# A two-layer graph kernel issued in a hand-written order: new due times for every step, and the last bias row added to the residual on GpSimd

## The chip, the core and the metric

The kernel runs on one core of a Trainium2 chip. Five engines work beside each other, each through its own queue of instructions in order: TensorE (PE in the profile, with its weight loads shown apart as PEld), VectorE (DVE), ScalarE (ACT), GpSimd (POOL) and SyncE (SP), which here only issues transfers. They wait for each other by semaphores. The metric is the device time of one execution in microseconds, lower is better.

## The reference, cut to what matters

128 graphs of 128 nodes with 64 features each pass through two layers. Both end in a layer normalization of the layer's input plus the layer's output.

```python
# layer 0: x (128, 128, 64), adj (128, 128, 128)
mask = (adj > 0.0).astype(x.dtype)
W1a, W1b = (W1[:F], W1[F:])                      # F = 64, H = 192, O = 64
diff = x[:, :, None, :] - x[:, None, :, :]
h = relu((x @ W1a)[:, :, None, :] + diff @ W1b + b1)
hm = jnp.einsum('bjkh,bjk->bjh', h, mask)
x = _layernorm(x + hm @ W2 + deg[..., None] * b2)
# layer 1
agg = jnp.einsum('bmn,bnd->bmd', adj, x)
h = elu(agg @ W1 + b1)
h = elu(h @ W2 + b2)
x = _layernorm(x + h @ W3 + b3)
```

The names W1 to W3 and b1 to b3 of layer 1 are v1, v2, v3 and c1, c2, c3 in the kernel.

## The kernel before

**Tiling.** A round handles one pair of graphs; there are 64 rounds (p = 0 to 63), and several are in flight at once. In each graph the nodes are sorted by their number of neighbours, so that a block of similar nodes needs the same number of neighbour slots. There are nine blocks (units) for a pair. For each unit ACT copies the node's own part into one of four PSUM banks e (L910), TensorE adds the neighbours' part by 18 bf16 matmuls with a one-hot matrix oh, alternating between the two halves of the array's columns (the gather, L920), and DVE reduces the absolute values into sums (L930). The gathers are 162, 66, 168, 112, 168, 154, 169, 154 and 170 columns wide; they are called by these widths here.

**Steps of a round on TensorE, with their lines.** Transposes of adj and x (turn, L690 and L691; ACT copies the result to turned, L695). The spread of the degrees (prepare, L248 or L246; DVE ranks them at L568 and makes the permutation permb at L575). The sorting of the mask (L246, copied by ACT to mtp and permT, L659 and L661) and its prefix sums (L248 with the operand prefix, copied by ACT to vp, L668), from which DVE makes the nine oh (L675). The sorting of x (L592, copied to xsT, L596), the node's own projection (L606, copied with its bias to aj by three ACT instructions, L613) and a short correction (L626, L629, used by DVE at L635 for ea). The neighbour projection (L708 with the bias matmul L711), split into three bf16 terms cp by ACT, DVE and POOL (L718 to L727). Then finish, the chain that closes a pair: POOL subtracts a correction (hm, L842), TensorE projects (L847, L851), ACT copies ys (L855), TensorE undoes the sorting (L864), norm makes x1 = the normalized result of layer 0; layer 1 follows with L871 (copied to agg, L875), L880, elu, L886, elu, and last (L891, L893), whose result goes through norm again to the output o and its transfer.

**PSUM.** Four banks e serve the gathers. Four banks m serve all other steps in turn; a step takes the bank that came free first, so its first matmul also waits for the last reader of that bank.

**norm and last.** norm adds the residual `rest` to the PSUM result on DVE (y, L737), takes bn_stats (st, L742), has POOL make the factors (ve, rs and, for layer 0, nb; L749 to L753) and ACT apply them (L771). In layer 1 the bias c3 is not part of rest. The matmul L891 adds it in PSUM: a matrix of ones times rowp, where rowp holds the row c3 (twice, with its mean removed) as three bf16 terms on three partitions. The f32 row itself, on all partitions, is the tile rows.

**What sets the order.** Nobody waits for a scheduler at run time: the program is written in the order in which the class Flow emits it, and each engine executes its part in this order. Every step belongs to a thread (prepare, sort_x, sort_mask, turn, project_c, finish, unit), and has a due time in the table DUE, in units of a model's microseconds from the beginning of its round; a round's beginning is ROUND * p with ROUND = 11.1651. While the gathers are under way (all units except the last 14), Flow emits of all threads' next steps the one with the earliest due time:

```python
            if self.under_way:
                t, th = min(ready, key=lambda r: self._rank(r[1]))
```

For the first steps and the last 14 units it takes the step that its clock model finds ready first. A step is a tuple of engine, cost, events to come after, number of banks m, and the function that emits it. The costs move only that clock; they aren't waited for on the chip. SP issues the loads of a pair four rounds ahead (AHEAD), and the output.

Of the kernel before, what the change touches and what calls it, by code (L numbers as in the profile page):

```python
# [31 lines left out]
F32 = mybir.dt.float32  # L32
# [154 lines left out]
def sparse(tc, env):  # L187

    g = type("env", (), dict(env))
    nc, P, N, F, H, O, HB, H1, NP, E = (  # L190
        g.nc, g.P, g.N, g.F, g.H, g.O, g.HB, g.H1, g.NP, g.E)
    LAY, NB = g.LAY, g.NB
    loads, prep, work, ps_m = g.loads, g.prep, g.work, g.ps_m
# [9 lines left out]
    AHEAD = 4  # L203

    DUE = {
        "prepare": (-42.67, -37.79, -37.67, -37.41, -37.15),
        "sort_x": (-21.11, -18.03, -15.85, -13.03, -12.9, 2.76, 2.89, 3.02, 3.14),
        "sort_mask": (-28.04, -27.66, -27.27, -15.21, -14.95, -14.31, -14.05, -13.8, -13.54,
                      -13.28, -3.02, -2.76, -2.5, -2.25),
        "turn": (-38.05, -37.92),  # L210
        "project_c": (-31.63, -29.71, -29.58, -29.45, -29.32, -17.13, -13.15),
        "finish": (12.51, 20.73, 21.24, 21.37, 21.5, 21.88, 22.01, 27.91, 28.3, 28.68, 32.02,
                   34.97, 35.1, 35.23, 41.26, 41.39, 43.95, 44.08, 46.78, 46.91, 54.48, 54.61,
                   59.48),
        "unit": [(0.06, 0.19, 0.32), (0.83, 0.96, 1.09), (0.45, 0.58, 0.71), (2.37, 2.5, 2.63),
                 (3.27, 3.4, 3.53), (4.43, 4.56, 4.68), (4.81, 4.94, 5.07), (5.33, 5.71, 6.1),
                 (7.64, 10.97, 11.1)],
    }

    def begin_thread(name, p, gen):  # L220
# [15 lines left out]
    def dve(n):  # L236
        return 0.08 + n / 960
# [12 lines left out]
    def flat(t):  # L250
        return t.rearrange("p s n -> p (s n)")
# [65 lines left out]
    def made(*names):  # L317
        return [event("const", name) for name in names]
# [410 lines left out]

    LATE = NP - 1  # L730

    def norm(p, yps, ev, name, rest, shift):


        y = work.tile([P, 2, O], F32, name="y", bufs=6)
        ev, = yield ("DVE", dve(2 * O), [ev], 0,
                     lambda: nc.vector.tensor_add(flat(y), yps[:, :2 * O], flat(rest)))  # L737
        flow.give(yps, ev)
        st = work.tile([P, 2, 3], F32, name="st", bufs=12)

        ev, = yield ("DVE", 0.2, [ev], 0,
                     lambda: nc.vector.bn_stats(st.rearrange("p s t -> p (s t)"),  # L742
                                                y.rearrange("p s f -> p f s")))
        ve = work.tile([P, 2], F32, name="ve", bufs=12)
        rs = work.tile([P, 2], F32, name="rs", bufs=12)
        nb = work.tile([P, 2], F32, name="nb", bufs=12) if shift else None

        def factors():
            nc.gpsimd.tensor_scalar(ve, st[:, :, 2], 1.0 / F, EPS, op0=OP.mult, op1=OP.add)  # L749
            nc.gpsimd.tensor_tensor(rs, ve, mhalf, op=OP.pow)  # L750
            if shift:
                for s in range(2):
                    nc.gpsimd.tensor_scalar(nb[:, s:s + 1], st[:, s, 1:2], rs[:, s:s + 1], -1.0,  # L753
                                            op0=OP.mult, op1=OP.mult)

        def variance():
            nc.vector.tensor_scalar(ve, st[:, :, 2], 1.0 / F, EPS, op0=OP.mult, op1=OP.add)

        def center(s):
            nc.vector.tensor_scalar(o[:, s, :], y[:, s, :], st[:, s, 1:2] if shift else 0.0,  # L760
                                    rs[:, s:s + 1], op0=OP.subtract, op1=OP.mult)
        if p < LATE:
            ev, = yield ("POOL PORT", 1.27 if shift else 0.97, [ev] + made("mhalf"), 0, factors)
        else:
            ev, = yield ("DVE", 0.1, [ev], 0, variance)
            ev, = yield ("POOL", 0.7, [ev] + made("mhalf"), 0,
                         lambda: nc.gpsimd.tensor_tensor(rs, ve, mhalf, op=OP.pow))
        o = work.tile([P, 2, F], F32, name=name, bufs=6)

        def apply(s):  # L770
            nc.scalar.activation(o[:, s, :], y[:, s, :], AF.Identity,  # L771
                                 bias=nb[:, s:s + 1] if shift else 0.0, scale=rs[:, s:s + 1])
        if p < LATE:
            ev, = yield ("ACT", 0.6 if shift else 0.46, [ev], 0, lambda: [apply(s) for s in range(2)])
        elif shift:
            ev, = yield ("DVE", 0.4, [ev], 0, lambda: [center(s) for s in range(2)])
# [25 lines left out]
    def overflow():  # L802
# [29 lines left out]
        ev, = yield ("DVE", 0.2, [ev], 0, lambda: v.tensor_reduce(some, t[:1, :B], AX.X, OP.max))  # L832
        flow.give(t, ev)

    def finish(p):

        d, xx = S[p], XX[p]
        hm = work.tile([P, 3, N], F32, name="hm")
        late = p >= LATE
        ev, = yield ("DVE PORT" if late else "POOL PORT", 0.47 if late else 1.05,  # L840
                     [event("corr", p)] + [event("sums", p, i) for i in range(NB)], 0,
                     lambda: (nc.vector if late else nc.gpsimd).tensor_sub(hm, d["sums"], d["corr"]))  # L842

        def project(yb):
            cp, mtp = d["cp"], d["mtp"]
            for c in range(3):
                nc.tensor.matmul(yb[:, :2 * O], hm[:, c, :], flat(w2d[:, c]),  # L847
                                 start=(c == 0), stop=False)
            for s in range(2):
                for i in range(3):  # L850
                    nc.tensor.matmul(yb[:, s * O:(s + 1) * O], mtp[:, s, :], cp[:, i, s, H:H + O],  # L851
                                     start=False, stop=(s == 1 and i == 2))
        ev, yb = yield ("PE", 0.85, [ev] + made("w2d"), 1, project)
        ys = work.tile([P, 2 * O], F32, name="ys")
        ev, = yield ("ACT", act(2 * O), [ev], 0, lambda: nc.scalar.copy(ys, yb[:, :2 * O]))  # L855
        flow.give(yb, ev)
        if p == NP - 1:
            due = DUE["finish"]
            flow.start(ROUND * p, [due[4]] * 4 + [due[8], due[12], due[12], due[14], due[15], due[15]],
                       overflow())  # L860

        def unsort(t):
            for s in range(2):
                nc.tensor.matmul(t[:, s * O:(s + 1) * O], d["permT"][:, s, :],  # L864
                                 ys[:, s * O:(s + 1) * O], start=True, stop=True)
        ev, t = yield ("PE", 0.4, [ev, event("permT", p)], 1, unsort)
        x1, ev = yield from norm(p, t, ev, "x1", xx, True)

        def aggregate(t):
            for s in range(2):  # L870
                nc.tensor.matmul(t[s * F:(s + 1) * F, :N], x1[:, s, :], d["turned"][:, s, :],  # L871
                                 start=True, stop=True)
        ev, t = yield ("PE:t", 0.22, [ev, event("turned", p)], 1, aggregate)
        agg = work.tile([P, N], F32, name="agg")
        ev, = yield ("ACT", act(N), [ev], 0, lambda: nc.scalar.copy(agg, t[:, :N]))  # L875
        flow.give(t, ev)

        def hidden1(zb):
            for s in range(2):
                nc.tensor.matmul(zb[:, s * N:(s + 1) * N], v1p[:, s, :], agg,  # L880
                                 start=True, stop=True)
        ev, zb = yield ("PE", 0.49, [ev] + made("v1p"), 1, hidden1)
        h1, ev = yield from elu(zb, ev, "h1", 0)

        def hidden2(zb):
            nc.tensor.matmul(zb[:, :2 * N], v2s, h1, start=True, stop=True)  # L886
        ev, zb = yield ("PE", 0.48, [ev], 1, hidden2)
        h2, ev = yield from elu(zb, ev, "h2", 1)

        def last(t):  # L890
            nc.tensor.matmul(t[:, :2 * O], onesb[:, :P], c3p, start=True, stop=False)  # L891
            for s in range(2):
                nc.tensor.matmul(t[:, s * O:(s + 1) * O], h2[:, s * N:(s + 1) * N], v3s,  # L893
                                 start=False, stop=(s == 1))
# [284 lines left out]
```

## Time and profile before

| | us |
|---|---|
| median of 3 runs | 772.05 (771.89 to 772.5) |
| the profiled execution | 772.32 |
| its span, first to last instruction | 770.6 |
| one round in the middle of the run | 11.395 |
| first gather's second matmul starts at | 30.68 |
| last gather ends, about | 749.4 |

The granted TensorE clock is 0.985 on average. The span is what the profile shows of the execution; 1.7 us lie around it. A start-to-start distance is the time from the start of one instruction to that of the next on the same engine; where neither waits, it is what the instruction costs its engine, while the duration in the profile also holds the part that overlaps the next. The matmul's end in the profile is modelled, so its start and the start of its weight load are the times to trust. An f32 matmul appears as two instructions.

Busy times of the engines in two rounds in the middle of the run, a view of stretches:

```profile
411.10:422.50 11.40, 11.40 (x235) 10.46 (x232) 11.08 (x38) 10.98 (x32) 6.62 (x13) 1.00 0.11 27
422.50:433.89 11.39, 11.39 (x235) 10.45 (x232) 11.07 (x38) 10.97 (x32) 6.61 (x13) 1.00 0.11 26
```

The columns after the window are its length, and busy time with the number of instructions for PE, PEld, DVE, ACT and POOL; then the granted clock, the share of the DMA engines and GB/s. The rounds repeat to within a few nanoseconds.

POOL's and DVE's instructions that the change is near to:

| line | what | mean ns |
|---|---|---|
| L737 | y, DVE, 128 x 128 | 275 to 286 |
| L742 | bn_stats, DVE | 289 |
| L727 | third term of cp, POOL, 128 x 512 | 1162 |
| L842, L620, L642 | f32 two-input operations, POOL, 128 x 384 | 1002 to 1021 |
| L363 | f32 subtraction, POOL, 128 x 64 | 306 |
| L891 | bias matmul, PE, 128 columns bf16 | 222 |

### The profile page before, as it was taken

What the parts mean: (1) busy time and instruction counts of PE and PEld (TensorE: products, weight loads), DVE (VectorE), ACT (ScalarE), POOL (GpSimd) and SP (SyncE); (2) the same over time, 40 slices, a digit from 0 to 9 for tenths busy, and PEclk for the clock granted to TensorE, in tenths of its full rate; (3) what the DMA queues carried; (4) which work ended last, traced back from release to release, by engine and by line L of the source; (5) the groups of instructions that cost most, each with busy time, mean ns of one, the idle gap of its engine ahead of it and who ended that gap; (6) DMA issues with size and microseconds to landing.
All of it is one profiled execution on the core that took longest, in us unless ns stands there. A gap on an engine that the chain in (4) does not pass through costs nothing.

```text
span 770.6 us, 36007 instructions
## 1 busy us (share of the span) xinstructions
PE 746.3 (97%) x14616; PEld 679.5 (88%) x14617; DVE 725.2 (94%) x2381; ACT 705.5 (92%) x1986; POOL 430.1 (56%) x801
## 2 busy tenths in 40 slices
PE   7599999999999999999999999999999999999995
PEld 5489999999999999999999999999999999999993
DVE  6699999999999999999999999999999999999994
ACT  5479999999999999999999999999999999999984
POOL 5145565565565565556556556556555655655652
PEclk9699999999999999999999999999999999999997
DMA  4000010110110011011011011011101101100000
GB/s 123 11 3 3 17 30 17 30 31 20 27 30 23 24 31 30 16 31 30 17 30 30 17 30 31 21 26 31 30 17 30 31 16 31 31 17 19 11 10 21
DMA packets 54668, 19.70 MB, mean 26 GB/s; under 512 B 37601, under 2 KB 54497, under 8 KB 54497
## 3 DMA queue, kind: packets, MB, share of 16 engines
q1 hardware_dynamic: 53792, 17.05, 9.1%
q8 instruction: 116, 1.90, 1.0%
q14 instruction: 56, 0.45, 0.2%
q10 hardware_dynamic: 704, 0.30, 0.2%
HBM read 13.14 MB, written 4.19 MB: 22 GB/s over the span
## 4 chain that ended last, share of the span: by engine, by line
PE 94%; DVE 3%; ACT 2%; issue 0%; DMA 0%; POOL 0%; ACTq 0%; POOLq 0%; DVEq 0%
PE e L920 45%; PE m L606 6%; PE m L708 5%; PE m L847 5%; PE m L880 4%; PE m L886 4%; PE m L864 4%; PE m L893 4%; PE m L690 3%; PE m L248 2%; PE m L871 2%; PE m L592 2%; PE m L246 2%; PE m L851 1%; PE m L711 1%; PE m L691 1%
## 5 line engine op out<-in xcount | busy, mean ns | idle before, releaser
L920 PE MATMUL e<-oh,cp 128*64 128x162 bf16 (+3 forms) x10368 | 392.7, 229 | 6.2 <-DVE oh L675 5.2
L920 PEld LDWEIGHTS <-cp 128*64 128x64 bf16 x10368 | 356.9, 110 | 15.3 <-issue 6.9
L930 DVE TENSOR_REDUCE sums<-e 128x54 f32<-128x486 f32 (+8 forms) x576 | 327.1, 609 | 16.7 <-PE m L629 9.9
L910 ACT COPY e<-aj 128x504 f32<-128x504 f32 (+6 forms) x576 | 293.3, 540 | 9.5 <-DVE sums L930 8.9
L749 POOL TENSOR_SCALAR ve<-st 128x2 f32<-128x2 f32 x126 | 24.1, 191 | 254.1 <-DVE st L742 246.9
L675 DVE TENSOR_TENSOR oh<-vp,slotc 128x308 bf16<-128x308 bf16 (+6 forms) x576 | 137.3, 314 | 0.8 <-ACT vp L668 0.6
L750 POOL TENSOR_TENSOR rs<-ve,mhalf 128x2 f32<-128x2 f32 x126 | 87.8, 696 | 10.5
L727 POOL TENSOR_TENSOR cp<-r,cp 128x512 bf16<-128x512 f32 x64 | 74.4, 1162 | 18.6 <-ACT cp L725 18.6
L642 POOL TENSOR_TENSOR corr<-ea,sa 128x384 f32<-128x384 f32 x64 | 64.2, 1003 | 32.8 <-DVE ea L635 32.8
L842 POOL TENSOR_TENSOR hm<-sums,corr 128x384 f32<-128x384 f32 x63 | 63.1, 1002 | 5.8 <-DVE sums L930 5.8
L620 POOL TENSOR_TENSOR sa<-aj,srow 128x384 f32<-128x384 f32 x64 | 65.4, 1021 | 0.0
L797 DVE SCALAR_TENSOR_TENSOR h<-m,cc,e 128x256 f32<-128x256 f32 x128 | 60.8, 475 | 3.8 <-ACT e L794 3.6
L791 ACT ACTIVATE r<-m,cc 128x256 f32<-128x256 f32 x128 | 61.3, 479 | 2.4 <-PE m L886 2.4
L606 PEld LDWEIGHTS m<-xsT,wad 128*128 128x128 f32 x384 | 48.3, 193 | 13.0 <-ACT turned L695 11.8
L613 ACT ACTIVATE aj<-m,b1c 128x128 f32<-128x128 f32 x192 | 57.2, 386 | 2.3 <-PE m L606 2.3
L606 PE MATMUL m<-xsT,wad 128*128 128x128 f32 x384 | 58.4, 289 | 0.6 <-DVE r L722 0.6
L794 ACT ACTIVATE e<-r 128x256 f32<-128x256 f32 x128 | 53.3, 418 | 2.0
L847 PE MATMUL m<-w2d,hm 128*128 128x128 f32 x384 | 53.4, 276 | 0.0
L722 DVE TENSOR_TENSOR r<-m,cp 128x256 f32<-128x256 f32 x128 | 47.8, 415 | 2.8 <-ACT cp L718 2.8
L771 ACT ACTIVATE x<-y,nb,rs 128x64 f32<-128x64 f32 x126 | 48.9, 439 | 1.4 <-POOL nb L753 1.4
L847 PEld LDWEIGHTS m<-w2d,hm 128*128 128x128 f32 x384 | 48.1, 192 | 0.1
L708 PE MATMUL m<-wc,turned 64*128 64x256 f32 x256 | 46.3, 436 | 0.9 <-DVE r L722 0.9
(159 smaller groups left out, 1350.5 us busy)
## 6 DMA issues: line engine op xcount, KB each, us to landing
adj<-in_adj_dram SPq DMA_DIRECT2D x64, 128.0 KB, 2.4
xx<-in_x_dram SPq DMA_DIRECT2D x64, 64.0 KB, 2.2
out_dram<-o SPq DMA_DIRECT2D x64, 64.0 KB, 1.6
w1s<-in_L_gnn_W_dram ACTq DMA_DIRECT2D x2, 96.0 KB, 2.8
w2s<-in_L_gnn_W_dram ACTq DMA_DIRECT2D x2, 48.0 KB, 2.7
v2s<-in_L_gnn_W_dram SPq DMA_DIRECT2D x1, 64.0 KB, 2.3
v1d<-in_L_gnn_W_dram SPq DMA_DIRECT2D x2, 32.0 KB, 2.0
rows<-in_L_gnn_b_dram SPq DMA_DIRECT2D x1, 64.0 KB, 4.8
```

The costliest lines, as they stand in the source:

```text
L606: nc.tensor.matmul(aps[:, c * N:(c + 1) * N], wad[:, c, :], xsT, start=True, stop=True)
L620: evs, = yield ("POOL PORT", 1.0, [have] + made("srow"), 0, lambda: nc.gpsimd.tensor_mul(sa, aj, srow))
L642: ev, = yield ("POOL PORT", 1.05, [ev, evs], 0, lambda: nc.gpsimd.tensor_sub(corr, ea, sa))
L675: lambda: nc.vector.tensor_tensor(oh[:, :, c].rearrange("p b (s w) -> p b s w", w=w), vp[:, :, p0:p1].rearrange("p b (o w) -> p b o w", o= ...
L708: nc.tensor.matmul(cps[s][:, :cols], d["turned"][k, 2, :], wc[k, :], start=True, stop=False)
L727: lambda: nc.gpsimd.tensor_sub(cp[:, 2], r1, cp[:, 1]))
L750: nc.gpsimd.tensor_tensor(rs, ve, mhalf, op=OP.pow)
L842: lambda: (nc.vector if late else nc.gpsimd).tensor_sub(hm, d["sums"], d["corr"]))
L847: nc.tensor.matmul(yb[:, :2 * O], hm[:, c, :], flat(w2d[:, c]), start=(c == 0), stop=False)
L910: lambda: nc.scalar.copy(e.rearrange("p (c s w) -> p c s w", c=3, w=w), d["aj"][:, :, p0:p1].rearrange("p c (o w) -> p c o w", o=1) .to_br ...
L920: nc.tensor.matmul(e[s * HB:(s + 1) * HB, c * n:(c + 1) * n], cp[:, k, s, c * HB:(c + 1) * HB], oh[:, s, base:base + n], start=False, stop ...
L930: nc.vector.tensor_reduce(d["sums"][:, :, p0:p1], e.rearrange("p (c s w) -> p c w s", c=3, w=w), AX.X, OP.add, apply_absolute_value=True)
```

## The change

Three parts.

1. In last, the bias matmul L891 goes; the two matmuls with v3s open and close their own groups.
2. A new thread, residual, is started as soon as x1 is known. Its one step adds rows to x1 on POOL, into a new tile x1c with 4 buffers, due at 32.7. The second norm takes x1c as its rest, and its y step waits for that event as well.
3. All due times in DUE are new, except ROUND, so every engine's instructions stand in another order.

```diff
     DUE = {
-        "prepare": (-42.67, -37.79, -37.67, -37.41, -37.15),
+        "prepare": (-43.06, -42.93, -39.21, -39.08, -35.87),
...
-        "finish": (12.51, 20.73, 21.24, 21.37, 21.5, 21.88, 22.01, 27.91, 28.3, 28.68, 32.02,
-                   34.97, 35.1, 35.23, 41.26, 41.39, 43.95, 44.08, 46.78, 46.91, 54.48, 54.61,
-                   59.48),
-        "unit": [(0.06, 0.19, 0.32), (0.83, 0.96, 1.09), (0.45, 0.58, 0.71), (2.37, 2.5, 2.63),
+        "finish": (12.64, 19.44, 19.57, 21.62, 21.75, 21.88, 22.01, 28.04, 28.17, 29.2, 33.56,
+                   33.69, 33.82, 34.71, 43.31, 43.44, 44.47, 44.6, 46.52, 46.65, 48.06, 48.19,
+                   59.87),
+        "residual": (32.7,),
+        "unit": [(-1.48, 0.96, 1.09), (2.12, 2.25, 2.37), (3.02, 3.14, 3.27), (3.66, 3.79, 3.91),
...
-    def norm(p, yps, ev, name, rest, shift):
+    def norm(p, yps, ev, name, rest, shift, *after):
...
-        ev, = yield ("DVE", dve(2 * O), [ev], 0,
+        ev, = yield ("DVE", dve(2 * O), [ev, *after], 0,
...
+    def residual(p, x1, x1c, ev):
+
+        ev, = yield ("POOL PORT", 0.45, [ev] + made("rows"), 0,
+                     lambda: nc.gpsimd.tensor_add(flat(x1c), flat(x1), rows))
+        happened(ev, "x1c", p)
...
         x1, ev = yield from norm(p, t, ev, "x1", xx, True)
+        x1c = work.tile([P, 2, F], F32, name="x1c", bufs=4)
+        flow.start(ROUND * p, DUE["residual"], residual(p, x1, x1c, ev))
...
         def last(t):
-            nc.tensor.matmul(t[:, :2 * O], onesb[:, :P], c3p, start=True, stop=False)
             for s in range(2):
                 nc.tensor.matmul(t[:, s * O:(s + 1) * O], h2[:, s * N:(s + 1) * N], v3s,
-                                 start=False, stop=(s == 1))
+                                 start=True, stop=True)
...
-        o, ev = yield from norm(p, t, ev, "o", x1, False)
+        o, ev = yield from norm(p, t, ev, "o", x1c, False, event("x1c", p))
```

The steps of one round in the middle of the run, as they stand on TensorE (named by the lines of the kernel before; gathers by their widths):

| before | after |
|---|---|
| L690, L691 | L690, L691 |
| L248 spread, L248 prefix, L886, L606 | L606 |
| L847, L851 | L847, L851 |
| L880, L864 | L886, L248 prefix, L864, L880 |
| gathers 170, 162, 168, 66 | gather 170, L592, gather 162 |
| L708, L711, L891, L893 | L708, L711, L893 |
| gather 112, L626, L629 | gather 66, L626, L629 |
| gather 168, L592, gathers 154, 169 | gathers 168, 112, 168, 154 |
| L246 sorting, gather 154, L871 | L246 spread, L871, gathers 169, 154, L246 sorting |

On POOL the new order is corr, ve and rs of the output's norm, cp, the new x1c, ve, rs and nb of x1's norm, hm, the two small degree operations, sa. On DVE one round reads: ea; sums 168; bn_stats of the output; sums 112; the two differences for cp (L722); sums 168 and 154; the two rankings; sums 169 and 154; oh for 154 and 66; permb; six more oh; oh for 162, which reads the vp just made; y of x1; its bn_stats; h2; sums 170 and 162; h1; the two mask operations (L545); y of the output; sums 66. The chain that makes rowp stays in the program, for the dense path that runs only when a pair overflows its slots.

More of the change, by code (lines that the diff above doesn't have):

```diff
@@ L205, in sparse @@
     DUE = {
-        "prepare": (-42.67, -37.79, -37.67, -37.41, -37.15),
[L207 to L211, printed above, removed]
-        "finish": (12.51, 20.73, 21.24, 21.37, 21.5, 21.88, 22.01, 27.91, 28.3, 28.68, 32.02,
-                   34.97, 35.1, 35.23, 41.26, 41.39, 43.95, 44.08, 46.78, 46.91, 54.48, 54.61,
-                   59.48),
-        "unit": [(0.06, 0.19, 0.32), (0.83, 0.96, 1.09), (0.45, 0.58, 0.71), (2.37, 2.5, 2.63),
-                 (3.27, 3.4, 3.53), (4.43, 4.56, 4.68), (4.81, 4.94, 5.07), (5.33, 5.71, 6.1),
-                 (7.64, 10.97, 11.1)],
+        "prepare": (-43.06, -42.93, -39.21, -39.08, -35.87),
+        "sort_x": (-26.76, -10.46, -10.33, -3.14, -3.02, 2.5, 2.63, 2.76, 2.89),
+        "sort_mask": (-26.12, -25.99, -25.86, -23.42, -23.29, -23.16, -13.67, -13.28, -13.03,
+                      -12.77, -2.63, -2.25, -1.99, -1.73),
+        "turn": (-36.9, -36.77),
+        "project_c": (-32.15, -29.32, -29.2, -29.07, -28.94, -4.17, -4.04),
+        "finish": (12.64, 19.44, 19.57, 21.62, 21.75, 21.88, 22.01, 28.04, 28.17, 29.2, 33.56,
[3 more added lines that the diff above has]
+        "unit": [(-1.48, 0.96, 1.09), (2.12, 2.25, 2.37), (3.02, 3.14, 3.27), (3.66, 3.79, 3.91),
+                 (4.68, 4.81, 4.94), (5.07, 5.2, 5.33), (5.97, 6.1, 6.22), (6.35, 6.48, 6.61),
+                 (7.25, 11.61, 11.74)],
     }
```

## The prediction

> **What bounds the kernel now.** I read the page first (busy times, the chain that ended last), then the waits, then the timelines of TensorE, its weight loads (PEld) and ACT over one round. A round (one pair of batches) takes 11.395 us: the same line starts again after that time in 56 of the 63 steps between rounds, from 72 to 710 us. The profiled execution took 772.32 us, 770.6 of it span.
>
> From the page:
>
> ```profile
> span 770.6 us, 36007 instructions
> ...
> PE 746.3 (97%) x14616; PEld 679.5 (88%) x14617; DVE 725.2 (94%) x2381; ACT 705.5 (92%) x1986; POOL 430.1 (56%) x801
> ...
> PE 94%; DVE 3%; ACT 2%; issue 0%; DMA 0%; POOL 0%; ACTq 0%; POOLq 0%; DVEq 0%
> ```
>
> TensorE sets the end. But busy matmuls are not matmuls at their peak: a weight load that waits is hidden behind the modelled end of the matmul before it. One such wait shows in the list of waits (total, times, longest), and the timelines of one round (start, duration, engine, line, operation, out<-in, size, count, idle before it) show two more by their starts:
>
> ```profile
> PEld m L606 <- ACT turned L695: 11.8, 57, 0.2
> ```
>
> ```profile
> 412.61 0.27 PE L248 MATMUL m<-mtp,prefix 128*128 128x256 bf16 x1
> 412.72 0.65 PE L886 MATMUL m<-h,v2s 128*128 128x256 f32 x2
> 413.21 0.91 PE L606 MATMUL m<-xsT,wad 128*128 128x128 f32 x6
> ...
> 414.62 0.34 PE L851 MATMUL m<-cp,mtp 128*128 128x64 bf16 x6
> 414.79 0.69 PE L880 MATMUL m<-agg,v1p 128*128 128x128 f32 x4
> 415.32 0.65 PE L864 MATMUL m<-ys,permT 128*128 128x64 f32 x4
> 415.90 2.44 PE L920 MATMUL e<-oh,cp 128*64 128x170 bf16 x72
> ...
> 418.97 0.22 PE L891 MATMUL m<-rowp,onesb 128*128 128x128 bf16 x1
> 419.02 0.61 PE L893 MATMUL m<-v3s,h 128*128 128x64 f32 x4
> ```
>
> ```profile
> 412.67 0.30 PEld L886 LDWEIGHTS m<-h,v2s 128*128 128x128 f32 x2
> 413.18 0.74 PEld L606 LDWEIGHTS m<-xsT,wad 128*128 128x128 f32 x6 [0.21 <-ACT turned L695]
> 415.31 0.52 PEld L864 LDWEIGHTS m<-ys,permT 128*128 128x128 f32 x4
> 418.94 0.10 PEld L891 LDWEIGHTS <-onesb 128*128 128x128 bf16 x1
> 418.97 0.53 PEld L893 LDWEIGHTS m<-v3s,h 128*128 128x128 f32 x4
> ```
>
> ```profile
> 412.35 0.27 ACT L596 COPY xsT<-m 128x128 f32<-128x128 f32 x1
> 412.64 0.48 ACT L695 COPY turned<-m 128x384 f32<-128x384 f32 x1
> 414.99 0.27 ACT L855 COPY ys<-m 128x128 f32<-128x128 f32 x1
> ```
>
> Elsewhere a load starts 2 ns after the matmul before it starts. Three loads start 0.05 us after an ACT copy ends instead. L886 waits for xsT (412.62): its two matmuls stand 270 ns apart, not the 216 of an unhindered 256-column f32 pass: 54 ns lost. L606 waits for turned (413.12): 182 ns, not 112: 70 lost. L864 waits for ys (415.26): the last matmul of L880 starts at 415.21, so 100 lost. Sum 0.224 us a round; unhindered, this order needs 11.395 - 0.224 = 11.171.
>
> **What the Trainium skill says.** "TensorE: Matmul & The Clock Gate", step-by-step part, lets the queue pull a weight load ahead of matmuls in flight; so a load costs only what is longer than the matmul it runs behind. Its section on LDWEIGHTS gives columns/1.2, 107 ns for 128; f32 loads here follow each other at 110 to 112. Its section on weight-path modes says 128-column non-f32 loads are faster; the trace has 29 (418.94 to 418.97). "SBUF — State Buffer", who interferes with whom: a VectorE instruction with two SBUF inputs and a GpSimd one that reads SBUF exclude each other for the whole instruction. The nine oh (L675) are of that kind; in the round shown POOL rests during them (oh 413.92 to 416.06, POOL idle from 412.44 to 416.36), so no run here shows the collision.
>
> **The change part by part**, per round, on TensorE.
> 1. Bias matmul gone. It streams 57 ns (418.97 to 419.02), but the 110 ns f32 load of L893 runs behind it. Without it that load starts 29 ns earlier, behind L711, and then stands bare. Nearest case: once in the drain (745.0 us) a 64-column f32 matmul follows a short bf16 one, L851 to L864, and reaches its second start 28 + 140 = 168 ns later; L711 over L891 to the second start of L893 takes 29 + 57 + 111 = 197. So 29 saved, not 57; bounds 0 (all hidden) to 57.
> 2. L880 now stands last before the gathers, not L864. Before a gather the array drains: 123 ns pass after the start of a 64-column bf16 matmul (L711, early rounds), its stream of 27 and 96 more; 205 after L864's last, which is 54 of a load still running, a stream of 53 and 98. The eight matmuls cost 112 each in either order; only the last stream lies bare, and for 128 f32 columns it is 107, not 53: +53 (bounds 0 to 60).
> 3. The spread of the degrees (L248, 3 x 56 = 168) becomes six half-width matmuls among gathers, three pairs at 57: +3. L592, L871, L626, L629 and the gathers only change places; the column streams add up as before.
> 4. The waits. The new order puts L606 right behind L691; its bank was last read by agg, whose ACT copy (my layout, below) ends 1.2 us earlier: 0. L886 moves behind L851 and waits for turned, 0.7 us early: 0. L864 gets L886 and L248 in front of it instead of L880. From the last L851 matmul its load would start 0.54 us later (110 load + 216 + 216), not 0.45; ys was ready at 0.55. Stall 0.00 to 0.01, from 0.100.
>
> Sum: 11.171 - 0.029 + 0.053 + 0.003 = 11.198; 0.197 less than 11.395, times 56 = 11.0 us. So nearly all comes from the reordering.
>
> This holds if nothing else is late. I laid one round of the new order on all engines with start-to-start distances from the trace, time 0 at L690.
> ACT: turned 0.65 to 1.12, aj behind L606 (1.26), ys 2.10, vp 3.13, xsT 4.64, then without a pause to the copy for the 169-column gather, done 9.33, needed 9.58. That 0.25 is the smallest margin of a gather.
> DVE: its 29 groups add up to 10.91, with one new own wait (bn_stats right behind its y, 0.12) inside and about 0.07 on a gather. It starts at 3.56 with oh for 162, which waits for vp, and is back there at 14.54: 0.2 spare in 11.20. h2 is done 4.85, its bank needed by L708 at 5.15; h1 6.40, needed by L626 at 6.74.
> POOL: 7.4 of 11.2. The new add of 128 elements costs 0.45 (from 64: 0.305, 384: 1.00; the page has no 128), behind cp (10.82 to 11.94), ahead of ve at 15.6. Its reader, the output y, comes at 17.9: it hides behind that 5 us. Behind it on POOL wait only ve, rs and nb. DVE's new wait for it has h1 and mk ahead of it, and the sums for the 66-column gather and all later sums behind.
> Constants: rows is f32 and made before rowp already; SP's issues keep their order; rowp and its constant chain stay for the unused dense path. The first gather still waits for all nine oh behind that chain (PE idle 4.9 us before 30.68). Fill and drain chains keep their length; I allow 1 us either way.
>
> So span 770.6 - 11.0 = 759.6, execution about 761.3; the median shown is 0.27 under the profiled execution: **761.0 us**.
>
> **Rivals.**
> A, the wait grows back: ys has no margin, aj sits ahead of it on ACT. If ys, the 169 copy or h2 are late by 0.1 a round, half is lost: 11.30, 766.7. For it: three ACT waits exist now. Against: the margins above, 0.25 except ys.
> B, slower: oh and the new add exclude each other. The add would end at 12.39 and the first oh start at 12.45, so they touch. If oh comes first, the add waits up to 2 us, which its cover of 5 us takes. Up to 0.2 of blocking DVE absorbs; from there it bounds. The whole 0.45 on top of 10.98 gives 11.43: 774.0. If cp too slid onto oh (1.16), 12.14 and 814; for that ACT would have to be 0.6 late.
> C, only the bias matmul counts and all three waits come back elsewhere: 11.198 + 0.224 = 11.42, 773.5. Against: each wait's partner was looked up in the new order.
> D, the change as described does less: 64 matmuls and loads are gone and 64 adds are there; but what the title names is worth 1.6 us (56 x 0.029), or 3.2 if I mis-sized it.
>
> **How the numbers follow.** Forecast 0.72 (own range 759.3 to 763.5: period 11.18 to 11.24, ends 1 us); A 0.12; B 0.10; C 0.06. The range 759 to 767 holds the forecast's case and most of A's; B and C, 0.16, lie above it, and some of the forecast's ends below or above its own range. A measurement of this kernel tells 0.2% (1.5 us) from no change. Faster: 0.72 + 0.12 = 0.84; of C 0.03 within, 0.03 above; B above: same 0.03, slower 0.13.
>
> **What would show it.** A period of 11.20 between starts of L606; no PEld wait at L606; no weight load that starts just after an ACT copy ends; the first two matmuls of L893 near 140 ns apart; DVE with a short wait for vp each round; POOL's new add ended before the first oh. Wrong if DVE's oh last longer or start late while POOL reads, or if L711 to L893 saves its full 57.

## The result, and the profile after

| | before | changed |
|---|---|---|
| median of the runs shown | 772.27 us | 759.66 us (759.28 to 760.08) |
| ratio, 95% interval | | 0.9835 (0.9820 to 0.9851) |
| span of the profiled execution | 770.6 us | 758.3 us |
| distance between rounds, steady | 11.395 us | 11.212 us |

The forecast was 761.0. From the page after (span, busy time of each engine, shares of the chain that ended last):

```profile
span 758.3 us, 36113 instructions
...
PE 735.9 (97%) x14724; PEld 670.9 (88%) x14725; DVE 723.3 (95%) x2381; ACT 706.4 (93%) x1986; POOL 459.6 (61%) x865
...
PE 94%; DVE 1%; DMA 1%; ACT 1%; SPq 1%; issue 0%; POOL 0%; POOLq 0%; DVEq 0%
```

TensorE still sets the end, and its busy share did not move: 97% before, 97% after. What changed stands in the starts of one round. The changed kernel has other line numbers: its L607, L709, L712, L854, L858, L895, L249, L871, L889, L880, L901 and L928 on TensorE are L606, L708, L711, L847, L851, L886, L248, L864, L880, L871, L893 and L920 of the kernel before, and its oh (L676 on DVE) is L675. From the timeline of the changed kernel (start us, duration, engine, line, operation, out<-in, size, count), TensorE's full-width stretch and the output layer:

```profile
402.77 0.83 PE L607 MATMUL m<-xsT,wad 128*128 128x128 f32 x6
403.44 0.83 PE L854 MATMUL m<-w2d,hm 128*128 128x128 f32 x6
404.11 0.34 PE L858 MATMUL m<-cp,mtp 128*128 128x64 bf16 x6
404.28 0.68 PE L895 MATMUL m<-h,v2s 128*128 128x256 f32 x2
404.80 0.27 PE L249 MATMUL m<-mtp,prefix 128*128 128x256 bf16 x1
404.91 0.56 PE L871 MATMUL m<-ys,permT 128*128 128x64 f32 x4
405.30 0.66 PE L889 MATMUL m<-agg,v1p 128*128 128x128 f32 x4
405.89 0.85 PE L928 MATMUL e<-oh,cp 128*64 128x170 bf16 x18
...
408.17 0.23 PE L712 MATMUL m<-b2p,onesb 128*128 128x64 bf16 x2
408.23 0.64 PE L901 MATMUL m<-v3s,h 128*128 128x64 f32 x4
```

The same for the weight loads, and for ACT's copies:

```profile
402.66 0.75 PEld L607 LDWEIGHTS m<-xsT,wad 128*128 128x128 f32 x6
404.25 0.30 PEld L895 LDWEIGHTS m<-h,v2s 128*128 128x128 f32 x2
404.80 0.52 PEld L871 LDWEIGHTS m<-ys,permT 128*128 128x128 f32 x4
408.21 0.53 PEld L901 LDWEIGHTS m<-v3s,h 128*128 128x128 f32 x4
```

```profile
403.02 0.50 ACT L696 COPY turned<-m 128x384 f32<-128x384 f32 x1
404.48 0.27 ACT L862 COPY ys<-m 128x128 f32<-128x128 f32 x1
407.02 0.27 ACT L597 COPY xsT<-m 128x128 f32<-128x128 f32 x1
```

The three waits are gone, but for a trace of one. L607's loads run from 402.66 with nothing to wait for: its six starts stand 558 ns apart in all (629 before), and the list of waits has no entry for a load of L607. L895's first load starts 2 ns behind the last start of L858. L871's load alone still carries the sign of a wait: it starts 51 or 52 ns behind the end of ys (404.75) in every one of 55 rounds. But this is only 2 to 7 ns behind the start of L249, so some 5 ns are lost there at most, and not 100. ys comes just in time, with nothing to spare.

POOL and DVE around the new addition, in the same round:

```profile
403.11 0.46 POOL L839 TENSOR_TENSOR x1c<-x,rows 128x128 f32<-128x128 f32 x1
403.65 0.47 DVE L676 TENSOR_TENSOR oh<-vp,slotc 128x308 bf16<-128x308 bf16 x2
```

The addition ends at 403.57, 0.08 us ahead of the first oh. In 48 of 50 rounds this gap lies between 0.05 and 0.09 us; once it is 0.15, and once there is none.

**Where the 12.3 us went.** Fifty-six steady steps of 0.183 us are 10.2 us. The rest comes from the two ends. At the start the gather that waits for all oh of the first round comes 3.1 us earlier. From the timelines of the kernel before and of the changed one:

```profile
24.14 0.15 DVE L508 TENSOR_TENSOR cc<-cc,m 128x1 f32<-128x1 f32 x1 [0.88 <-PE m L505]
...
30.68 3.14 PE L920 MATMUL e<-oh,cp 128*64 128x162 bf16 x53 [4.92 <-DVE oh L675]
```

```profile
20.21 0.15 DVE L509 TENSOR_TENSOR cc<-cc,m 128x1 f32<-128x1 f32 x1 [0.66 <-ACT e L918]
...
27.56 1.38 PE L928 MATMUL e<-oh,cp 128*64 128x162 bf16 x17 [5.57 <-DVE oh L676]
```

The wait is not shorter (in brackets: idle before, and who ended it), but the constant chain that stands ahead of the oh on DVE begins at 20.21 and not at 24.14. Where the steady rounds begin, the changed kernel leads by 4.3 us (the gather of 162 columns at 70.45 and not at 74.75), where they end by 14.5 (698.31 and not 712.85), and at the end of the span by 12.3. So the start gave 4.3 us, and 2.3 were given back behind the steady rounds.

### The profile page after: what moved, and what is told of

It is laid out like the page before. It is cut to its first block, busy times and chain, and to the rows that moved or that the text cites. A ratio compares the mean times of both kernels' runs of the same rounds, so it can differ in the third digit from the quotient of the medians.

```text
span 758.3 us, 36113 instructions
## 1 busy us (share of the span) xinstructions
PE 735.9 (97%) x14724; PEld 670.9 (88%) x14725; DVE 723.3 (95%) x2381; ACT 706.4 (93%) x1986; POOL 459.6 (61%) x865
## 4 chain that ended last, share of the span: by engine, by line
PE 94%; DVE 1%; DMA 1%; ACT 1%; SPq 1%; issue 0%; POOL 0%; POOLq 0%; DVEq 0%
PE e L928 47%; PE m L607 6%; PE m L854 6%; PE m L709 5%; PE m L895 4%; PE m L889 4%; PE m L901 4%; PE m L871 3%; PE m L247 3%; PE m L691 3%; PE m L880 2%; PE m L593 2%; PE m L858 1%; PE m L712 1%; PE m L692 1%; PE m L249 1%
## 5 line engine op out<-in xcount | busy, mean ns | idle before, releaser
L928 PE MATMUL e<-oh,cp 128*64 128x162 bf16 (+3 forms) x10368 | 393.2, 229 | 6.0 <-DVE oh L676 5.6
L928 PEld LDWEIGHTS <-cp 128*64 128x64 bf16 x10368 | 357.7, 110 | 18.6 <-issue 6.9
L938 DVE TENSOR_REDUCE sums<-e 128x54 f32<-128x486 f32 (+8 forms) x576 | 334.1, 608 | 7.6 <-PE e L928 4.3
L676 DVE TENSOR_TENSOR oh<-vp,slotc 128x308 bf16<-128x308 bf16 (+6 forms) x576 | 149.4, 315 | 4.5 <-ACT vp L669 0.9
L607 PE MATMUL m<-xsT,wad 128*128 128x128 f32 x384 | 53.7, 276 | 0.0
L854 PE MATMUL m<-w2d,hm 128*128 128x128 f32 x384 | 53.5, 275 | 0.0
L719 ACT CAST cp<-m 128x256 bf16<-128x256 f32 x128 | 40.2, 365 | 8.7 <-PE m L712 8.7
L607 PEld LDWEIGHTS m<-xsT,wad 128*128 128x128 f32 x384 | 47.9, 192 | 0.3
L854 PEld LDWEIGHTS m<-w2d,hm 128*128 128x128 f32 x384 | 48.0, 192 | 0.1
```

The source lines that it names most:

```text
L607: nc.tensor.matmul(aps[:, c * N:(c + 1) * N], wad[:, c, :], xsT, start=True, stop=True)
L676: lambda: nc.vector.tensor_tensor(oh[:, :, c].rearrange("p b (s w) -> p b s w", w=w), vp[:, :, p0:p1].rearrange("p b (o w) -> p b o w", o= ...
L928: nc.tensor.matmul(e[s * HB:(s + 1) * HB, c * n:(c + 1) * n], cp[:, k, s, c * HB:(c + 1) * HB], oh[:, s, base:base + n], start=False, stop ...
L938: nc.vector.tensor_reduce(d["sums"][:, :, p0:p1], e.rearrange("p (c s w) -> p c w s", c=3, w=w), AX.X, OP.add, apply_absolute_value=True)
```

## The experiments

To keep starts and ends apart from the rounds, each profile is cut in three: the start of the gather of 162 columns in round 5 (counted from 0), the mean distance of rounds 5 to 55, and the stretch from this gather in round 55 to the end of the span. First + 50 x distance + last is the span.

| kernel | median us | ratio to before, 95% | round 5 | distance | behind round 55 |
|---|---|---|---|---|---|
| before | 771.7 to 772.3 | 1 | 86.14 | 11.395 | 114.71 |
| changed | 759.66 | 0.9835 (0.9820, 0.9851) | 81.66 | 11.212 | 116.08 |
| old_order_add | 773.65 | 1.0017 (1.0010, 1.0023) | 85.68 | 11.365 | 117.75 |
| new_order_bias | 758.89 | 0.9837 (0.9824, 0.9851) | 80.69 | 11.240 | 114.16 |
| h1_before_unsort | 756.35 | 0.9789 (0.9770, 0.9807) | 82.20 | 11.158 | 115.55 |
| rows_late | 759.43 | 0.9845 (0.9832, 0.9859) | 81.12 | 11.212 | 115.97 |
| old_order_h2_late | 792.94 | 1.0270 (1.0256, 1.0284) | 87.17 | 11.724 | 118.33 |
| h2_late_behind_copy | 764.69 | 0.9905 (0.9890, 0.9921) | 85.33 | 11.228 | 115.92 |
| add_thrice | 760.30 | 0.9838 (0.9824, 0.9851) | 81.45 | 11.223 | 116.69 |
| add_six | 811.75 | 1.0512 (1.0497, 1.0526) | 82.89 | 12.063 | 124.98 |
| tail_bias | 759.08 | 0.9835 (0.9821, 0.9848) | 80.53 | 11.212 | 115.32 |
| rowp_spread | 757.63 | 0.9813 (0.9800, 0.9827) | 79.17 | 11.212 | 116.13 |
| old_consts_early | 769.49 | 0.9971 (0.9958, 0.9984) | 83.74 | 11.394 | 114.18 |
| swap_rowp | 753.72 | 0.9763 (0.9750, 0.9777) | 78.38 | 11.158 | 115.68 |

The distances repeat to some 3 ns from round to round, but for a few rounds of the two kernels with more additions. The column of round 5 and the last one carry 1 to 2 us of chance; what the runs show of its reason is said at the end.

### The two halves of the change, each alone

old_order_add takes the table of due times of before, with a place for the addition behind cp, and only what the title says of the bias row (the title's part, below):

```diff
+        "residual": (31.65,),
...
-            nc.tensor.matmul(t[:, :2 * O], onesb[:, :P], c3p, start=True, stop=False)
...
-        o, ev = yield from norm(p, t, ev, "o", x1, False)
+        o, ev = yield from norm(p, t, ev, "o", x1c, False, event("x1c", p))
```

> The old order on every engine, with only the title's part: no bias matmul L891, the bias row added to the residual by POOL right behind cp, x1c read by the output y. Theory (a removed bias matmul saves the 29 ns by which L893's first load starts earlier): period 11.366 us instead of 11.395, 64 x 0.029 = 1.9 us less, 770.4 against 772.3. Rival (its whole 57 ns counts): 3.6 us less, 768.6. Rival (the title's part carries the gain and the order only accompanies it): near 760.

new_order_bias is the changed kernel with these lines put back and without the addition.

> The new order on every engine, with the bias matmul kept and no addition on POOL. Theory (the order carries the gain): period 11.212 + 0.029 = 11.241 us, 1.9 us over the changed kernel, 761.5. Rival (57 ns): 763.3. Rival (the title's part carries the gain): near 771.

The distances came out at 11.365 and 11.240: the bias matmul is worth 29 ns in the old order and 28 in the new one, not its stream of 57. The times did not follow. old_order_add is slower than before by 0.17%, and new_order_bias no slower than the changed kernel: what the title's part saves in the rounds (1.6 us) does not reach the end of the profiled executions, where the last column grows by 3.0 us in the old order and by 1.9 in the new one. So the gain of the change is the order's; in the medians of whole runs the title's part is worth nothing, or a little less. In the new order this comparison isn't a clean one, though. Four of the five runs of new_order_bias had a mean granted clock of 0.988 or 0.989 (758.59 to 759.26 us) and the fifth 0.983 (761.09), while all four of the changed kernel had 0.983 or 0.984 (759.28 to 760.08). At a like clock the changed kernel is 1.0 to 1.8 us faster, by that one run.

### The order alone: taking away the waits by one move

old_order_h2_late leaves everything of before in place but hidden2 (L886), which goes between L880 and L864, and its relu on ACT, which goes right behind ys:

```diff
-                   34.97, 35.1, 35.23, 41.26, 41.39, 43.95, 44.08, 46.78, 46.91, 54.48, 54.61,
+                   34.97, 35.1, 35.23, 43.25, 43.6, 43.95, 44.08, 46.78, 46.91, 54.48, 54.61,
```

> The kernel before with one thread's step moved: L886 (hidden2) between L880 and L864 instead of ahead of L606, its relu behind ys on ACT; bias matmul, spread of the degrees and all else as before. Theory (the three hidden weight-load waits are what the new order removes): L606 takes over the bank that xsT frees and keeps the 54 ns wait for xsT, L847 takes the bank that turned frees and comes after it, L864 comes 0.4 us after ys is ready: 0.170 of the 0.224 us go, period 11.225 us, 772.0 - 56 x 0.170 = 762.5. Rival (the waits only move to the next line that takes the bank): 11.39 and 772. Rival (the h2 chain, now 1.4 us later, makes L893 wait): above 772.

It was slower than before: 11.724, and for a reason that none of the three expectations has. On TensorE the expected happened (the starts of L847 stand 558 ns apart, those of L864 279 where it was 375, and only L606 keeps a wait of 50 for xsT). But in the timeline of ACT stands a wait that was not there:

```profile
413.15 0.29 ACT L855 COPY ys<-m 128x128 f32<-128x128 f32 x1
414.02 0.47 ACT L791 ACTIVATE r<-m,cc 128x256 f32<-128x256 f32 x1 [0.58 <-PE m L886]
```

relu comes to the head of ACT's queue 0.58 us before L886 is done, and the copies for the next gathers are queued behind it. ACT is busy for 11.04 us of this round and has no 0.58 us to give, so it became the bound. The second attempt puts relu one copy later, and the two steps behind it with it:

```diff
-                   34.97, 35.1, 35.23, 41.26, 41.39, 43.95, 44.08, 46.78, 46.91, 54.48, 54.61,
+                   34.97, 35.1, 35.23, 43.25, 44.76, 44.8, 44.84, 46.78, 46.91, 54.48, 54.61,
```

> As old_order_h2_late, which lost because h2's relu, put right behind ys, held ACT idle for 0.58 us a round until L886 was done; here relu and exp stand behind the copy for the 162-column gather, one copy later on ACT, so that L886 is done when they come. Theory (ACT had no room for the wait; the three TensorE waits themselves are worth what the trace shows): ACT does not wait at relu, period 11.225 to 11.26 us, 762 to 765. Rival (the h2 chain or a gather copy is late wherever relu stands): above 11.395, 772.

11.228, against 11.225 worked out from the two waits. So these two hidden waits are worth what the starts in the profile of before say, and taking them away needs a few steps of one thread moved and nothing else of the change. The third, the one for xsT, was not taken away alone: here L606 keeps some 50 ns of it, and it goes only in the changed kernel.

### What stands last before the gathers

h1_before_unsort is the changed kernel with one due time made earlier, so that L889 (hidden1) comes ahead of L871 (the unsorting):

```diff
-        "finish": (12.64, 19.44, 19.57, 21.62, 21.75, 21.88, 22.01, 28.04, 28.17, 29.2, 33.56,
+        "finish": (12.64, 19.44, 19.57, 21.62, 21.75, 21.88, 22.01, 28.04, 28.17, 29.2, 32.75,
```

> The changed kernel with L889 (hidden1) moved ahead of L871 (unsort) on TensorE, nothing else moved. Theory (the last matmul before the gathers lies bare with its stream, 107 ns for 128 f32 columns, 53 for 64): period 11.212 - 0.053 = 11.159 us, 3.0 us less, 756.7. Rival (the unsort's result, 0.4 us later, makes DVE's y late, or DVE has no room left below 11.21): period 11.21, 759.7, with a DVE wait at y. Rival (the drain does not depend on what stands last): 759.7 with the gap before the gather unchanged at 205 ns and no DVE wait.

11.158, 54 ns less. From the first start of these eight matmuls to the gather pass 986 ns in the changed kernel and 933 here. Read by the starts of the matmuls, the difference lies not behind the last start (205 ns to the gather either way) but inside L889, whose four starts stand 389 ns apart in the changed kernel and 335 here. The starts of the loads put it back in its place. A start in the record can come before the matmul's own load is done: L871's second start in the changed kernel stands 58 ns behind its first, while its load began 3 ns behind that first start and needs some 110. Counted with 110 ns a load, which is an estimate from the distances of the loads, the last load before the gather ends 1 ns behind the last start in the changed kernel (load at 405.578, start at 405.687) and 55 ns behind it here (404.625 and 404.680). That leaves 204 and 150 ns to the gather: a stream of 107 or of 53, and 97 more in both. DVE's y has no wait. This is the 53 ns that the change had paid for its order.

### Does the addition collide with the oh?

add_thrice and add_six repeat the addition with the same inputs and output:

```diff
-                     lambda: nc.gpsimd.tensor_add(flat(x1c), flat(x1), rows))
+                     lambda: [nc.gpsimd.tensor_add(flat(x1c), flat(x1), rows) for k in range(6)])
```

> The changed kernel with the new addition on POOL done three times in a row (same inputs, same output), so that 1.37 us of POOL instead of 0.457 stand from the end of cp, 0.9 us of them beside the first oh of DVE. Theory of rival B in the prediction (a DVE instruction with two SBUF inputs and a POOL instruction that reads SBUF exclude each other): the first oh last 0.4 to 0.5 us longer each where they meet an addition, 0.9 us of DVE lost, of which 0.15 to 0.25 is covered by its wait for vp: period 11.85 to 11.95, 796 to 801 us. Other theory (they only share bandwidth, or not even that): oh as long as before, period 11.212, 759.7.

> The changed kernel with POOL's new addition done six times. In add_thrice the two additions that met the oh cost DVE 0.31 us (oh of 66 columns 496 ns instead of 236, of 169 columns 383 instead of 338), and DVE's wait for vp took up all but 0.01. Theory (each waits for the other to end, and DVE has 0.15 to 0.25 us to give): five additions beside the oh cost DVE 0.8 us or more, period 11.75 or more, 790 or more. Rival (the loss is taken up by other waits too): period below 11.3, 765 or less.

Three additions left the distance at 11.212 in 47 of the 50 rounds; the mean is 0.011 higher because three rounds are 0.11, 0.15 and 0.30 us longer, and the cause of these is open. Yet the collision was there in every round: the oh of 66 columns took 0.50 us and not 0.24, the one of 169 columns 0.38 and not 0.34, and the addition beside the first 0.60 instead of 0.46. DVE lost 0.31 us a round and gave it from its own waits, that for vp (0.15) among them. Six additions lengthened five oh by 1.19 us together, more than DVE had to give: 12.063, 0.85 more. From the groups of DVE by shape (two batches of columns each, so 132 are 66), of add_six and then of the changed kernel (busy us, mean ns of one):

```profile
L676 DVE TENSOR_TENSOR oh<-vp,slotc 128x224 bf16<-128x224 bf16 x64 | 35.8, 560 | 0.0
L676 DVE TENSOR_TENSOR oh<-vp,slotc 128x132 bf16<-128x132 bf16 x64 | 31.2, 488 | 0.0
...
L676 DVE TENSOR_TENSOR oh<-vp,slotc 128x340 bf16<-128x340 bf16 x64 | 21.3, 332 | 0.0
```

```profile
L676 DVE TENSOR_TENSOR oh<-vp,slotc 128x340 bf16<-128x340 bf16 x64 | 21.2, 331 | 0.0
...
L676 DVE TENSOR_TENSOR oh<-vp,slotc 128x224 bf16<-128x224 bf16 x64 | 18.1, 284 | 0.0
L676 DVE TENSOR_TENSOR oh<-vp,slotc 128x132 bf16<-128x132 bf16 x64 | 15.6, 244 | 0.0
```

An oh that meets an addition lasts 0.04 us (169 columns) to 0.30 us longer; one that comes after the last addition (340) is as before. For three, the first theory had the mechanism right and the size wrong (0.65 to 0.75 expected, 0.01 measured): an addition cost DVE at most 0.3 us, not its whole 0.46, and DVE has room for 0.3. For six its 11.75 or more held.

### The start

rows_late spreads the last fourteen DVE instructions of the constant chain over rounds 1 and 2 instead of ahead of the first oh:

```diff
+        flow.start(14.0, range(14), consts_rows(c3, ev))
+
+    def consts_rows(c3, ev):
```

> The changed kernel, with the last fourteen DVE instructions of the constant chain (means of v3s and rows, the bf16 parts of rowp; 3.2 us of DVE from 22.89 to 26.09) spread behind the first oh instead of ahead of them. Theory (the start of the changed kernel is 3.7 us earlier than before because this chain begins earlier, and the rest of its length still holds the first gathers): the gather that waits until 27.56 starts 3.2 us earlier, 759.7 - 3.2 = 756.5, period unchanged at 11.212. Rival (something else, the cp planes or the second pair's sort, holds the first gathers at that time): 759.7.

The gather did start at 23.92, 3.6 us earlier, and the gathers of round 2 still 3.8 earlier (45.20 against 48.98), but those of round 3 only 0.5: round 2 took 13.97 us (10.74 in the changed kernel). So the time stayed at 759.43, as the rival had it, though not for the rival's reason. Seven of the moved instructions stand in round 2, where DVE is busy for 13.75 us. They take 3.4 us there and 1.6 at the start of the changed kernel: about half of the loss is that DVE has no room for them, the other half that three of them met POOL. The timelines of POOL and DVE of this kernel show two of these:

```profile
48.22 1.00 POOL L853 TENSOR_TENSOR hm<-sums,corr 128x384 f32<-128x384 f32 x1
...
49.52 0.99 POOL L625 TENSOR_TENSOR sa<-aj,srow 128x384 f32<-128x384 f32 x1
```

```profile
48.40 0.96 DVE L366 TENSOR_TENSOR low<-hm,mid 128x128 bf16<-128x128 f32 x1
...
49.56 1.00 DVE L367 COPY rowp<-hi 1x128 bf16<-1x128 bf16 x1
```

At the start of the changed kernel, beside an idle POOL, low took 0.29 us and the copy of one row 0.18. Here each lasts to just behind the end of the POOL instruction that it meets. rowp_spread moves only the seven instructions of rowp, one a round into rounds 8 to 14, ahead of the last oh, where DVE waits for vp and POOL rests. For this one of their scratch tiles gets memory of its own, x1c has 3 buffers and not 4, and only the last five pairs still wait for rowp:

```diff
-        for name, fn in parts(rows, rowp, NR):
+        flow.start(10.0, [ROUND * k for k in range(8, 15)], consts_rowp())
```

> The changed kernel, with only the seven DVE instructions that make rowp (which no matmul of the sparse path reads any more) moved from the start to rounds 8 to 14, one a round, into DVE's wait for vp ahead of the last oh, where POOL rests. Theory (they hold the first gathers, and beside the oh they cost nothing): the second gather starts 1.6 us earlier, period 11.212 but for up to 0.1 us in seven rounds, 758.1 to 758.5. Rival (time won ahead of the first gathers is lost again in rounds 1 and 2, as it was when the whole chain was spread there): 759.7.

The waiting gather starts at 25.52 and not at 27.56, the distance stays 11.212, and the gain lasts to the end: 757.63. That the beginning of the chain matters as much as its length was tried on the kernel before, by its due time alone:

```diff
-    flow.start(ROUND * -0.5, [0.0], consts_late())
+    flow.start(ROUND * -1.2, [0.0], consts_late())
```

> The kernel before, with the constant chain (sums of the weights on TensorE, then the DVE chain to rowp) placed earlier by its due time, so that its two matmuls stand ahead of a pair of L708 that waits for DVE and no longer behind it; from round 2 on nothing differs. Theory (the start is shorter in the changed kernel because this chain begins 3.9 us earlier): the wait of the first gathers ends 3.0 to 3.5 us earlier than at 30.68, period 11.395, 768.6 to 769.2. Rival (the new place of the units and sorts in the first rounds makes the difference): 772.

The chain begins at 20.66 and the gather starts at 28.89 (30.68 before), at an unchanged distance: 2.2 us less in the medians, 3.0 in the spans. 1.8 of the expected 3.0 to 3.5 show at the gather itself. The chain begins 3.5 us earlier, but from its begin to the first oh behind it pass 5.4 us and not 4.6, because two of its instructions meet POOL:

```profile
23.27 1.15 POOL L727 TENSOR_TENSOR cp<-r,cp 128x512 bf16<-128x512 f32 x1 [4.91 <-ACT cp L725]
23.40 1.10 DVE L364 CAST mid<-hm 128x128 bf16<-128x128 f32 x1
...
24.38 0.99 POOL L642 TENSOR_TENSOR corr<-ea,sa 128x384 f32<-128x384 f32 x1
24.54 0.98 DVE L365 TENSOR_TENSOR low<-hm,mid 128x128 bf16<-128x128 f32 x1
```

In the kernel before mid takes 0.23 us and low 0.29, and one instruction of the chain meets POOL (L510, 0.91 us). The other 0.9 us go to an oh and two r that had run ahead of the chain and now stand behind it.

### The end, and the two that paid together

tail_bias lets the last five pairs add their bias row by the matmul again.

```diff
+        with_matmul = p >= NP - 5
...
+            if with_matmul:
+                nc.tensor.matmul(t[:, :2 * O], onesb[:, :P], c3p, start=True, stop=False)
```

> The changed kernel, but the last five pairs add the bias row by the matmul as before and not on POOL. Theory (the title's part saves 29 ns in each of the steady rounds, and gives 2 to 3 us back after them, where TensorE's granted clock falls to half about 5 us earlier): period 11.212, the stretch behind the last steady round 2 us shorter, 757.6. Rival (the 2 us were chance of one execution): 759.7.

This one decides nothing: its runs lie between 757.65 and 760.10 and cover both expectations.

swap_rowp joins h1_before_unsort and rowp_spread.

> The changed kernel with both edits that paid: L889 ahead of L871, and the making of rowp spread over rounds 8 to 14. They touch different stretches, so they should add up: period 11.158, start as in rowp_spread, 759.7 - 3.0 - 2.0 = 754.7. Rival (DVE, with 0.05 us less room in a shorter round, no longer hides rowp): 755 to 757.

753.72, where 754.7 was expected: the two add up. This kernel is 2.4% faster than the kernel before and 0.8% faster than the changed one.

## Why the prediction was right, and where it was not

**Step 1, the bias matmul: right.** 29 ns forecast; 29 and 28 measured, each between two kernels that differ in the title's part alone. The first two starts of L901 stand 139 ns apart, against some 140 forecast.

**Step 2, the drain with L880 last: right.** 53 ns forecast, 54 won by undoing it; and counted from the starts of the loads it is the last stream that lies bare, as the prediction had it.

**Step 3 and the sum: 14 ns low.** The sum said 11.198, the trace 11.212. Of the 14 ns, 8 lie in the full-width stretch (3.508 us from the transposes to the gather, against 3.500 worked out) and 6 among the half-width matmuls, where the spread had been put at 3. Neither remainder has a shown cause, beyond the few ns for which L871's load waits for ys.

**Step 4, the waits: right.** All three are gone in the trace but for those few ns (0.00 to 0.01 us forecast), and h2_late_behind_copy gets two of them by another road, at the price that was read from the starts.

**The layout of the other engines held.** The addition takes 0.457 us (0.45 forecast) and ends 0.08 us ahead of the first oh; DVE waits 0.15 us for vp (0.2 forecast).

**The ends were the step that failed.** "Fill and drain chains keep their length; I allow 1 us either way": the start became 4.3 us shorter and 2.3 us were given back behind the steady rounds, so that the span came out 2.0 us better than the rounds alone and hid that the rounds gave 10.2 and not 11.0. That the total lies within 1.3 us of the forecast is in this much luck. The prediction saw the chain ahead of the first oh, but only asked whether it was still there, not when it starts.

**The rivals.** A did not come: no wait grew back by more than a few ns, though ys has no margin, as A feared. That such margins are thin is shown by old_order_h2_late, where one ACT wait of 0.58 us turned a gain of 0.17 into a loss of 0.33 a round. B's mechanism is real and its place is right. In the steady rounds it was kept away by some 0.07 us; behind them, in three pairs (58 to 60), the addition does meet oh and takes 0.53 to 0.61 us. From add_six one can read what it costs where it lands. A like collision stood already in the start of the kernel before, with an instruction of another kind: L510 on DVE took 0.91 us beside two of POOL, and 0.17 in old_consts_early, where it met none. The prediction, which went by the steady round, said that no run showed one. "SBUF — State Buffer" of the Trainium skill (two separate sides) says that whichever of the two starts first holds the shared ports for its whole instruction and the other blocks; the oh of add_six (up to 0.30 us longer) and the low of rows_late (0.96 us and not 0.29) agree with that. C is refuted by new_order_bias. D was right about the title: 1.6 us in the rounds, as it said. What the end makes of them is the open part.

**Still open** is the end. With the addition the stretch behind the last rounds is longer in both orders (3.0 and 1.9 us in the profiled executions), and the two differences lie in different places. In the old order 2.0 of the 3.0 us arise ahead of the last gather's last matmul (749.4), while the clock was still full (to 757.1). There the instructions of the last pairs stand in another order than before: for the last 14 units Flow takes the step that its clock model finds ready first, and the addition is a step more in it. In the new order the changed kernel gains 1.2 us up to the last gather and loses 2.0 from there to the last computing instruction, where its clock was at half from 743.5 and that of new_order_bias from 748.8. Another 1.15 us lie behind that instruction: from DVE's branch at the end to its next event pass 3.07 us in the changed kernel and some 0.6 in new_order_bias. No view names a cause, but it does not go with the addition: this time is 2.9 to 3.8 us in nine of the fourteen kernels, h2_late_behind_copy without any addition among them, and 0.6 in the other five, old_order_add among them. So whether the addition itself costs anything at the end isn't shown.

## What to carry to other kernels

In a queue bound by its own length, look for weight loads that start just behind another engine's copy: they can be waits which no idle time shows, and the distance of the starts prices them (11.225 us worked out, 11.228 measured). The sign alone is not enough: a load that also starts just behind the matmul before it loses nothing. Price a removed instruction by how much earlier the next load begins that nothing hides (29 ns), not by its own stream (57), and check the start and end of the program separately, since 1.6 us won in 56 rounds did not show in the whole. When a step is moved, ask what it holds up on the queue that it waits in: here a single early wait on a nearly full engine cost more than all that the move won.

## What the runs showed of the hardware

In the kept traces TensorE's granted clock is either full or half, and holds in steps of 3.41 us. At the start it was half for 13.65 us in the kernel before (from 20.4), for 10.24 in the changed one and for 6.83 in rowp_spread and tail_bias, four, three and two steps. At the end it fell at 761.1 before, at 757.1 in old_order_add, at 743.5 in the changed kernel and at 748.8 in new_order_bias. From the windows of the last two, at 740 to 750 us (PEclk is the third number from the end):

```profile
740.00:745.00 5.00, 3.21 (x19) 2.29 (x20) 3.81 (x18) 3.37 (x11) 3.81 (x9) 0.85 0.06 13
745.00:750.00 5.00, 4.43 (x21) 2.62 (x20) 2.12 (x8) 2.67 (x6) 0.00 (x0) 0.50 0.06 13
```

```profile
740.00:745.00 5.00, 3.87 (x34) 3.11 (x34) 3.75 (x20) 3.34 (x10) 2.16 (x5) 1.00 0.08 18
745.00:750.00 5.00, 2.40 (x15) 1.55 (x13) 2.41 (x8) 3.36 (x10) 1.76 (x4) 0.88 0.06 13
```

The same four matmuls of L889 last 0.71 us at 742.37 and 1.23 at 744.39 in the changed kernel, which is why its busy PE rises in the second line. "TensorE: Matmul & The Clock Gate" of the Trainium skill (what's actually happening) describes such a gate, with two speeds and a window of about 3.4 us; the steps of 3.41 agree. The steps do not begin at a fixed point of the program (the first full one at 13.02 us in the changed kernel, at 14.16 in tail_bias, whose start is the same), and at the start and the end one step more or less at half speed falls by chance, as far as these runs show. The runs of old_order_add lie at 771.8 to 771.9 us where the mean clock was 0.987 and at 772.7 to 774.2 where it was 0.982 to 0.984; those of h1_before_unsort fall in order from 758.15 at 0.979 to 754.18 at 0.990. The kernel before does not show it: its 25 runs beside old_order_add lie at 771.3 to 772.8 with clocks from 0.982 to 0.988, in no such order.

Unexpected, too, was in rows_late that a copy of a single row of 128 bf16 elements on DVE (0.18 us alone) took 1.00 us beside a POOL multiplication of 0.99.
